# GpSimd's row additions ahead of a tanh: tensor-scalar with a per-partition scalar in place of tensor-tensor with a broadcast operand

## The chip, the cores and the metric

The kernel runs on one core of a Trainium2 chip. The metric is the device time of one execution in microseconds (us), the median of several runs. Beside it stands one execution taken by the hardware profiler, whose span is some microseconds shorter than the timed runs. The engines are called PE (TensorE), ACT (ScalarE), DVE (VectorE), POOL (GpSimd) and SP (SyncE, which issues DMAs). Every tensor is float32.

## What is computed

The input x has 8 batches of 64 x 16 = 1024 tokens with 128 channels. Layer 0 is an attention block with 8 heads, two softmaxes in a row on each score matrix, a feed-forward block and two layer norms. Layer 1 is an additive attention followed by a recurrence. The change is in the additive attention, whose heart is this:

```python
Wi = jnp.einsum('bnd,ed->bne', B, W)
scores = jnp.einsum('d,bijd->bij', v, jnp.tanh(Wi[:, None, :, :] + Wi[:, :, None, :]))
attn = jax.nn.softmax(scores, axis=-1)
```

For each of the 1024 tokens i of a batch, a row of Wi is added to all rows j, the tanh of every sum is taken, and the result is multiplied by v and summed over the 128 channels d. That is 1024 x 1024 x 128 tanh values per batch. The scores are symmetric in i and j, so the kernel computes only the blocks with j not before i, and gets the rest by transposing. After the attention, a linear recurrence through a sigmoid runs over the tokens; it stands at the end of the kernel and is not touched.

## The kernel before

**Tiling.** Channels lie on the 128 partitions and tokens along the free axis. `wiT` holds Wi of one batch in this form, 128 x 1024. Adding row i of Wi to all rows is then adding one column of `wiT`, a value per partition, to a 128 x w piece of `wiT`. The tokens i are cut into 8 tiles `it` of 128. For tile `it` only the w = 1024 − 128·it columns from its diagonal on are computed. Tiles 0 to 3 (w from 1024 to 640) are the wide ones; tiles 4 to 7 are the narrow ones.

**Groups.** `group` (from L930 on) adds the work of one group to the plan. A group takes k rows from each of the four 32-row quarters c of a tile, so 4k rows in all, with k = max(1, 1024 // w): one for the wide tiles, two for w = 512 and 384, four and eight for the last two tiles. Each row drops the columns ahead of its own diagonal (`begin`). A group lives in one of three buffers `th`, each 128 x 4096, and passes three steps:

1. *Fill.* Either ScalarE does addition and tanh in one instruction per row (`tanh_row`, L955, with the row's value as bias), or GpSimd or VectorE does only the additions. GpSimd does them by `add_rows` (L962), one tensor-tensor instruction per quarter c for its k rows, both operands broadcast views of `wiT`. VectorE does them by `add_row` (L958, tensor-scalar, one row each) for k under 4, else by `add_rows`.
2. *Tanh.* If the fill was only additions, ScalarE takes the tanh of the whole group in one instruction (L999).
3. *Product with v.* TensorE multiplies the rows with a pattern of v (L1016) and collects the scores of a tile in `sa`. This gives the `th` buffer free.

**Other work around it.** While batch b is in its layer-1 attention, layer 0 of batch b+1 is computed between: scores on TensorE (L820), exponentials on ScalarE (L823, L836), sums and divisions on VectorE (L827 to L840), and the second division on GpSimd (L843, a tensor-tensor with a broadcast operand, not changed). Transposes (L749) pass through PSUM banks that VectorE empties (L761), and L862 is the product with the values. Only layer 0 of batch 0 at the start, and the attention of batch 7 with the recurrence at the end, stand alone.

**What sets the order.** The kernel adds every piece of work to a `Plan`, with its engine or several engines to choose from, a cost in us for each, a priority and its dependences. `Plan.emit` runs a list scheduler over them when the kernel is built: it always takes the piece that can start earliest by these costs, within a small slack the one with the best priority, and puts it on an engine. So the costs in the table `work` decide which engine fills which group, and the order of every queue is fixed from then on. Pieces on GpSimd and those on VectorE that are marked `port` are planned so that they never overlap. For the wide tiles and the first narrow one, GpSimd is among the choices except for the last three groups of a tile; for the wide tiles, VectorE is among them only in the last batch.

Of the kernel before, what the change touches and what calls it, by code (L numbers as in the profile page):

```python
# [11 lines left out]
ALU = mybir.AluOpType  # L12
# [396 lines left out]
class Plan:  # L409
# [24 lines left out]
    def add(self, where, fn, r=(), w=(), pri=0, mode="full", take=None, give=None, behind=(), wait=(), port=False):  # L434
        n = len(self.ops)
        deps = set()
        for k in r:
            if k in self.writer:
                deps.add(self.writer[k])
        for k in (*w, *wait):  # L440
            if k in self.writer:
                deps.add(self.writer[k])
            deps.update(self.readers.get(k, ()))
        for k in w:
            self.writer[k] = n
            self.readers[k] = []
        for k in r:
            if k not in w:
                self.readers.setdefault(k, []).append(n)
        deps.discard(n)  # L450
        self.ops.append((where, fn, (pri, n), mode, deps, take, give, behind, port))
        self.by.append(None)
        return n
# [107 lines left out]
def fast_path(ctx: ExitStack, tc: tile.TileContext, a: dict, fits):  # L561
# [5 lines left out]
    nc = tc.nc  # L567
# [365 lines left out]
    def group(it, at0, r0, k, wiT, all_wi, L1, ROWS, fillers, chain, left, both):  # L933

        i0 = it * P
        w = N - i0
        g = count.setdefault("group", 0)  # L940
        count["group"] = g + 1
        slot = Bank(*slots)

        begin = [0 if r0 == 0 else 32 * c + r0 for c in range(4)]
        at = [k * sum(w - q for q in begin[:c]) for c in range(5)]

        def rows(c):
            return slot()[:, at[c] : at[c + 1]].rearrange("p (r n) -> p r n", r=k)

        def w_i(c, r=None):  # L950
            j = i0 + 32 * c + r0
            return wiT[:, j : j + k] if r is None else wiT[:, j + r : j + r + 1]

        def tanh_row(c, r):
            nc.scalar.activation(rows(c)[:, r, :], wiT[:, i0 + begin[c] :], AF.Tanh, bias=w_i(c, r))  # L955

        def add_row(c, r):
            nc.vector.tensor_scalar(rows(c)[:, r, :], wiT[:, i0 + begin[c] :], w_i(c, r), None, ALU.add)  # L958

        def add_rows(eng, c):  # L960
            shape = [P, k, w - begin[c]]
            eng.tensor_tensor(  # L962
                rows(c), wiT[:, i0 + begin[c] :].unsqueeze(1).to_broadcast(shape),
                w_i(c).unsqueeze(2).to_broadcast(shape), ALU.add,
            )


        each = [(c, r) for r in range(k) for c in range(4)]
        work = {
            "ACT": [(0.19 + 0.833e-3 * (w - begin[c]), lambda c=c, r=r: tanh_row(c, r)) for c, r in each],  # L970
            "POOL": [
                (0.25 + 1.7e-3 * k * (w - begin[c]), lambda c=c: add_rows(nc.gpsimd, c)) for c in range(4)
            ],
            "DVE": [(0.27 + 0.52e-3 * (w - begin[c]), lambda c=c, r=r: add_row(c, r)) for c, r in each]
            if k < 4
            else [(0.15 + 1.04e-3 * k * (w - begin[c]), lambda c=c: add_rows(nc.vector, c)) for c in range(4)],
        }

        def does(i):
            return lambda e: work[e][i][1]()  # L980

        first = count[chain] = add(
            [(e, work[e][0][0], x) for e, x in fillers], does(0), r=all_wi, w=[("rows", g, 0)], pri=ROWS,
            take=slot, behind=[count[q] for q in (chain, *both) if q in count], port=True,
        )

        def placed(i):
            def where():
                e = plan.by[first]

                return (e, work[e][i][0], -1.0 if e == "DVE" else 0.0) if i < len(work[e]) else None

            return where

        for i in range(1, 4 * k):
            add(placed(i), does(i), w=[("rows", g, i)], pri=ROWS, behind=[first], port=True)
        add(
            lambda: None if plan.by[first] == "ACT" else ("ACT", 0.2 + 0.833e-3 * at[4]),
            lambda _: nc.scalar.activation(slot()[:, : at[4]], slot()[:, : at[4]], AF.Tanh),  # L999
            r=[("rows", g, i) for i in range(4 * k)], w=[("tanh", g)], pri=ROWS - 0.02,  # L1000
        )


        parts = []
        for s0 in range(0, N, 512):
            for c in range(4):
                s, s1 = max(s0, at0 + begin[c]), min(s0 + 512, at0 + w)
                if s < s1:
                    parts.append((c, s0, s, s1))
                    left[c, s0] = left.get((c, s0), 0) + k  # L1010

        def times_v(_):
            for r in range(k):
                for c, s0, s, s1 in parts:
                    left[c, s0] -= 1
                    nc.tensor.matmul(  # L1016
                        sa[32 * c : 32 * c + 32, s:s1], vpat[:, 31 - r0 - r : 63 - r0 - r],
                        rows(c)[:, r, s - at0 - begin[c] : s1 - at0 - begin[c]],
                        start=at0 + r0 + r == 0, stop=left[c, s0] == 0,
                    )  # L1020

        n = -(-w // 512)
        before = ["sa"] if at0 and r0 == 0 else ["sa", "sa narrow"] if at0 else ["sa"] if r0 else []
        after = ["sa narrow"] if at0 and r0 == 0 else [] if r0 or at0 else ["sa"]
        add(
            ("PE", k * (1.67e-3 * (w - begin[0]) + 0.03 * n)), times_v, r=[("tanh", g)] + before,
            w=[("sa", it, r0)] + after, pri=L1, mode="groups", give=slot,
        )  # L1030
        return ("sa", it, r0)
# [11 lines left out]
    def layer1(b):  # L1043
# [19 lines left out]
        for n_pair, pair in enumerate(shared):  # L1063
# [16 lines left out]
            for s, it, at0, r0, k, fillers in sorted(todo):  # L1080
                ROWS = b + (n_pair + s / 33) / len(shared)
                L1 = ROWS - SOON
                keys.append(group(it, at0, r0, k, wiT, all_wi, L1, ROWS, fillers, fills[it < NT // 2], left, fills if r0 == 0 else ()))
# [188 lines left out]
    with tc.tile_pool(name="ps_w", bufs=2, space=PSUM) as ps_w, tc.tile_pool(  # L1272
# [26 lines left out]
        for g in range(NT // 4):  # L1299
            for b in range(NB):  # L1300
# [5 lines left out]
                eng = nc.sync if n % 2 else nc.scalar  # L1306
# [71 lines left out]
```

## Time and profile before

The median of 3 runs is 5963.16 us (5958.27 to 5963.76). The profiled execution has a span of 5955.2 us.

| engine | busy us | share of the span | instructions |
|---|---|---|---|
| PE | 5354.3 | 90% | 38755 |
| ACT | 5339.7 | 90% | 5305 |
| DVE | 4608.0 | 77% | 7127 |
| POOL | 3443.5 | 58% | 2186 |

The instructions that the change can touch, over the whole span:

| what | instructions | busy us | mean ns of one |
|---|---|---|---|
| L962 POOL, additions of a quarter | 1596 | 2397.4 | 1529 |
| L955 ACT, addition and tanh of a row | 3228 | 2434.9 | 821 |
| L999 ACT, tanh of a group | 695 | 1915.0 | 2771 |
| L958 DVE, addition of a row | 1244 | 597.2 | 547 |
| L962 DVE, additions of a quarter | 368 | 402.1 | 1154 |
| L843 POOL, second division | 512 | 997.4 | 1951 |

A busy time is the time in which at least one instruction of the group ran, while the mean is that of one instruction from its start to its end. Neighbours overlap a little, so busy time over count is below the mean. In a line of a group, the part after the second bar is the idle time of that engine just ahead of such instructions, and what ended most of it: "<-PE sa L1016 1008.2" says that the engine stood idle for 1008.2 us until a TensorE instruction of line 1016 was done. In a line of a window, the busy times stand in the order PE, PE's weight loads, DVE, ACT, POOL, with the number of instructions in brackets, and then the granted clock of TensorE and figures for DMA. The chain of waits follows the work that ended last back to the start, and gives each line's share of it.

### The profile page before, as it was taken

How to read it: one execution, taken by the hardware profiler on the slowest of the kernel's cores; microseconds unless marked ns; L12 is line 12 of the kernel's file. 1: busy time of each engine (PE TensorE's matmuls, PEld its weight loads, DVE VectorE, ACT ScalarE, POOL GpSimd, SP SyncE). 2: the span in 40 equal slices, each digit the busy share in tenths (PEclk: the TensorE clock that was granted, in tenths of full speed). 3: DMA queues.
4: the chain of work that ended last, by engine and by line, in shares of the span. 5: the costliest groups of instructions: out<-in, count | busy, mean ns of one | idle time of the engine just before them, and what ended most of it. 6: DMA issues, size and time to landing. Idle time of an engine off the chain costs nothing.

```text
span 5955.2 us, 96887 instructions
## 1 busy us (share of the span) xinstructions
PE 5354.3 (90%) x38755; PEld 3111.3 (52%) x38755; DVE 4608.0 (77%) x7127; ACT 5339.7 (90%) x5305; POOL 3443.5 (58%) x2186
## 2 busy tenths in 40 slices
PE   8989999999989998999999999999998999976667
PEld 5655555555555555455555555555554555532335
DVE  7897787878887778867788778887788777877754
ACT  5549999999998998999998999989999899989983
POOL 2338766786556766587655775568764767620000
PEclk9999999999999999999999999999999999989988
DMA  2000000000000000000000000000000000000001
GB/s 57 1 4 1 1 1 5 5 1 1 1 5 4 1 1 1 6 3 1 1 5 4 1 1 1 5 4 1 1 1 3 3 1 1 1 4 1 1 3 59
DMA packets 24301, 30.42 MB, mean 5 GB/s; under 512 B 2128, under 2 KB 18896, under 8 KB 23840
## 3 DMA queue, kind: packets, MB, share of 16 engines
q1 hardware_dynamic: 18736, 20.65, 1.1%
q8 instruction: 306, 5.01, 0.4%
q10 hardware_dynamic: 4944, 3.16, 0.2%
q14 instruction: 155, 1.27, 0.1%
q0 software_dynamic: 160, 0.33, 0.0%
HBM read 15.74 MB, written 8.39 MB: 4 GB/s over the span
## 4 chain that ended last, share of the span: by engine, by line
PE 52%; ACT 25%; DVE 16%; issue 6%; POOL 0%; DMA 0%; ACTq 0%; DVEq 0%; POOLq 0%
PE sa L1016 21%; ACT th L999 11%; ACT th L955 10%; PE m L862 9%; PE sc L820 9%; PE m L749 5%; DVE th L962 3%; DVE th L958 2%; ACT e L836 2%; ACT sc L823 2%; PE m L1124 2%; DVE aT L761 1%; PE sa L862 1%; DVE stat_e L839 1%; DVE stat_e L827 1%
## 5 line engine op out<-in xcount | busy, mean ns | idle before, releaser
L962 POOL TENSOR_TENSOR th<-wiT 128x1024 f32<-128x1024 f32 (+58 forms) x1596 | 2397.4, 1529 | 1310.8 <-PE sa L1016 1008.2
L955 ACT ACTIVATE th<-wiT 128x733 f32<-128x733 f32 (+61 forms) x3228 | 2434.9, 821 | 188.6 <-PE sa L1016 162.7
L1016 PE MATMUL sa<-th,vpat 128*32 128x512 f32 (+39 forms) x24576 | 2284.3, 474 | 292.7 <-ACT th L999 287.2
L999 ACT ACTIVATE th<-th 128x4096 f32<-128x4096 f32 (+48 forms) x695 | 1915.0, 2771 | 83.3 <-DVE th L958 40.5
L1016 PEld LDWEIGHTS sa<-th,vpat 128*32 128x32 f32 x24576 | 1033.7, 112 | 1352.8 <-issue 549.0
L843 POOL TENSOR_TENSOR e<-e,stat_e 128x1024 f32<-128x1024 f32 x512 | 997.4, 1951 | 882.8 <-DVE stat_e L840 698.2
L820 PE MATMUL sc<-xT,u 128*128 128x512 f32 x2048 | 987.5, 606 | 31.5 <-DVE e L831 28.9
L862 PE MATMUL m<-aT,vp 128*128 128x256 f32 x3664 | 891.9, 391 | 19.6 <-DVE aT L761 15.6
L862 PEld LDWEIGHTS m<-aT,vp 128*128 128x128 f32 x3664 | 677.2, 192 | 278.4 <-issue 109.4
L827 DVE TENSOR_REDUCE stat_e<-sc 128x16 f32<-128x1024 f32 x512 | 619.8, 1210 | 212.6 <-ACT sc L823 211.7
L839 DVE TENSOR_REDUCE stat_e<-e 128x64 f32<-128x1024 f32 x512 | 617.6, 1206 | 163.5 <-ACT e L836 161.4
L958 DVE TENSOR_SCALAR th<-wiT 128x384 f32<-128x384 f32 (+41 forms) x1244 | 597.2, 547 | 189.4 <-PE sa L1016 183.8
L761 DVE COPY aT<-m 128x512 f32<-128x512 f32 x906 | 587.1, 674 | 183.4 <-PE m L749 181.1
L831 DVE TENSOR_TENSOR e<-sc,stat_e 128x1024 f32<-128x1024 f32 x512 | 621.2, 1213 | 19.8 <-DVE stat_e L828 0.5
L749 PE MATMUL m<-ident,e 128*128 128x128 f32 x3796 | 558.7, 282 | 64.0 <-DVE aT L761 34.1
L823 ACT ACTIVATE sc<-sc 128x1024 f32<-128x1024 f32 x512 | 509.4, 1001 | 111.9 <-PE sc L820 111.6
L749 PEld LDWEIGHTS m<-ident,e 128*128 128x128 f32 x3796 | 420.4, 142 | 360.0 <-issue 177.9
L836 ACT ACTIVATE e<-e 128x1024 f32<-128x1024 f32 x512 | 534.1, 1046 | 51.1 <-DVE e L831 50.1
L820 PEld LDWEIGHTS sc<-xT,u 128*128 128x128 f32 x2048 | 357.1, 192 | 344.0 <-issue 288.5
L962 DVE TENSOR_TENSOR th<-wiT 128x1024 f32<-128x1024 f32 (+13 forms) x368 | 402.1, 1154 | 61.3 <-PE sa L1016 61.1
L840 DVE RECIPROCAL stat_e<-stat_e 128x64 f32<-128x64 f32 x512 | 283.2, 553 | 17.6
L718 POOL TENSOR_TENSOR stat<-stat,neg_half 128x4 f32<-128x4 f32 x64 | 67.6, 1056 | 227.7 <-DVE stat L715 225.9
(159 smaller groups left out, 2839.2 us busy)
## 6 DMA issues: line engine op xcount, KB each, us to landing
xT<-in_xt_dram SPq DMA_DIRECT2D x8, 512.0 KB, 3.6
th<-in_x_dram SPq DMA_DIRECT2D x8, 512.0 KB, 6.9
parked<-X SPq DMA_DIRECT2D x16, 256.0 KB, 2.0
xr<-parked SPq DMA_DIRECT2D x8, 512.0 KB, 7.0
out_dram<-ot ACTq DMA_DIRECT2D x8, 256.0 KB, 2.4
out_dram<-ot SPq DMA_DIRECT2D x8, 256.0 KB, 2.4
th<-in_wkn_dram ACTq DMA_DIRECT2D x1, 512.0 KB, 5.2
th<-in_wqn_dram SPq DMA_DIRECT2D x1, 512.0 KB, 5.0
```

Of the source, the lines that this page charges most:

```text
L749: nc.tensor.transpose(bank[:, i * P : (i + 1) * P], s, ident)
L820: nc.tensor.matmul(sc[:, cols], u[:, qt * P : (qt + 1) * P], xT[:, cols], start=True, stop=True)
L827: nc.vector.tensor_reduce(r1, sc.rearrange("p (m g) -> p g m", g=G), AX.X, ALU.add)
L836: add(("ACT", 1.05), lambda _, e=e: nc.scalar.activation(e, e, AF.Exp), r=[ke], w=[ke], pri=L0)
L839: nc.vector.tensor_reduce(r2, e3, AX.X, ALU.add)
L843: nc.gpsimd.tensor_tensor(e3, e3, r2.unsqueeze(2).to_broadcast([P, M, G]), ALU.mult)
L862: nc.tensor.matmul(bank()[:, :256], vp[:, t, :], aT[:, t, :], start=t == 0, stop=t == NT - 1)
L955: nc.scalar.activation(rows(c)[:, r, :], wiT[:, i0 + begin[c] :], AF.Tanh, bias=w_i(c, r))
L958: nc.vector.tensor_scalar(rows(c)[:, r, :], wiT[:, i0 + begin[c] :], w_i(c, r), None, ALU.add)
L962: eng.tensor_tensor(rows(c), wiT[:, i0 + begin[c] :].unsqueeze(1).to_broadcast(shape), w_i(c).unsqueeze(2).to_broadcast(shape), ALU.add,)
L999: lambda _: nc.scalar.activation(slot()[:, : at[4]], slot()[:, : at[4]], AF.Tanh),
L1016: nc.tensor.matmul(sa[32 * c : 32 * c + 32, s:s1], vpat[:, 31 - r0 - r : 63 - r0 - r], rows(c)[:, r, s - at0 - begin[c] : s1 - at0 - begin ...
```

## The change

GpSimd's entry in the table `work` is altered for k under 4, which is every group that GpSimd may take. It now adds row by row with a tensor-scalar instruction, whose second operand is one value per partition, in place of a tensor-tensor whose second operand is a broadcast column. So each instruction reads one stream of elements from SBUF rather than two. `add_row` gets the engine as an argument, so that GpSimd and VectorE share it. The planner's cost of a GpSimd row falls with it, from 1.7 to 0.9 ns an element; the fixed part stays at 0.25 us. Its aim is to make GpSimd's additions shorter, and with the new cost the planner distributes the groups over the engines anew.

```diff
-        def add_row(c, r):
-            nc.vector.tensor_scalar(rows(c)[:, r, :], wiT[:, i0 + begin[c] :], w_i(c, r), None, ALU.add)
+        def add_row(eng, c, r):
+            eng.tensor_scalar(rows(c)[:, r, :], wiT[:, i0 + begin[c] :], w_i(c, r), None, ALU.add)
...
             "POOL": [
-                (0.25 + 1.7e-3 * k * (w - begin[c]), lambda c=c: add_rows(nc.gpsimd, c)) for c in range(4)
-            ],
-            "DVE": [(0.27 + 0.52e-3 * (w - begin[c]), lambda c=c, r=r: add_row(c, r)) for c, r in each]
+                (0.25 + 0.9e-3 * (w - begin[c]), lambda c=c, r=r: add_row(nc.gpsimd, c, r)) for c, r in each
+            ]
+            if k < 4
+            else [(0.25 + 1.7e-3 * k * (w - begin[c]), lambda c=c: add_rows(nc.gpsimd, c)) for c in range(4)],
+            "DVE": [(0.27 + 0.52e-3 * (w - begin[c]), lambda c=c, r=r: add_row(nc.vector, c, r)) for c, r in each]
             if k < 4
             else [(0.15 + 1.04e-3 * k * (w - begin[c]), lambda c=c: add_rows(nc.vector, c)) for c in range(4)],
```

## The prediction

> **What bounds the kernel now.** I read the busy times of the page first, then the slices, a window over the middle, the chain of waits and each engine's waits in that window.
>
> ```profile
> PE 5354.3 (90%) x38755; PEld 3111.3 (52%) x38755; DVE 4608.0 (77%) x7127; ACT 5339.7 (90%) x5305; POOL 3443.5 (58%) x2186
> ```
> Two engines are nearly full, TensorE and ScalarE; GpSimd, whose instructions change, is not. The slices say where it works at all: hardly in the first two of 40, and not in the last four, where batch 7's attention is alone. So the stretch from 480 to 5200 us decides.
>
> ```profile
> 480.00:5200.00 4720.00, 4429.45 (x32656) 2547.74 (x32655) 3710.40 (x5514) 4476.98 (x4414) 3211.52 (x2043) 0.98 0.01 2
> ```
> Of 4720 us, PE is busy 4429 (94%), ACT 4477 (95%), DVE 3710 (79%), POOL 3212 (68%). The chain of waits and the groups of the same stretch:
>
> ```profile
> by line: PE sa L1016 24.3%; ACT th L955 11.6%; PE m L862 11.1%; PE sc L820 8.9%; ACT th L999 8.5%; PE m L749 5.6%; issue 4.0%; DVE th L962 3.2%; ACT e L836 2.2%; ACT sc L823 2.0%; DVE th L958 1.8%; PE m L1124 1.8%; DVE aT L761 1.3%; PE m L7
> ...
> L962 POOL TENSOR_TENSOR th<-wiT 128x1018 f32<-128x1018 f32 (+62 forms) x1556 | 2329.4, 1524 | 782.2 <-PE sa L1016 692.7 <-ACT th L955 40.9 <-DVE wiT L761 16.9
> L955 ACT ACTIVATE th<-wiT 128x308 f32<-128x308 f32 (+62 forms) x2965 | 2255.5, 828 | 146.7 <-PE sa L1016 121.8 <-DVE wiT L761 22.4
> L1016 PE MATMUL sa<-th,vpat 128*32 128x256 f32 (+40 forms) x20992 | 1904.9, 464 | 94.6 <-ACT th L999 89.2 <-ACT th L955 3.8
> L999 ACT ACTIVATE th<-th 128x4096 f32<-128x4096 f32 (+44 forms) x541 | 1487.5, 2756 | 63.5 <-DVE th L962 37.9 <-DVE th L958 21.6 <-POOL th L962 3.0
> ```
> The chain has no GpSimd piece among its leaders. PE never appears as waiting for POOL's rows; the big tanh (L999) waits for them 3 us. POOL itself waits 693 us for TensorE to give a buffer of th back. A faster GpSimd row by itself is therefore worth nearly nothing. What can pay is that, being cheap, GpSimd is given more groups, and ScalarE fewer instructions. TensorE waits for ScalarE 89.2 + 3.8 = 93 us here.
>
> **What the Trainium skill says.** "GPSIMD Engine Reference", section 4.1 (Engine selection), puts two-input elementwise work at about twice VectorE's time, because both inputs go through one read port, and calls one-input work "roughly line-rate"; section 1 gives 1.2 GHz. Line rate is then 0.83 ns an element, an estimate from that page. Section 3.1 has 2.6 cycles an element for two inputs. The trace disagrees in size: its tensor-tensor rows (below) take 1.55 ns, 1.9 cycles. Nearly two cycles for two reads fits the one port all the same. "SBUF — State Buffer", section Who interferes with whom: a GpSimd instruction shuts out VectorE instructions in the two-port mode (tensor-scalar) and those with two SBUF inputs for its whole length, and the other way round. The trace agrees in direction: the same VectorE row addition of 128x1024 takes 1220 ns in the median and 1501 ns in the mean.
>
> **The change, part by part.**
>
> *Price of the new instruction.* The trace has no GpSimd tensor-scalar. The nearest rows:
>
> ```profile
> L962 POOL TENSOR_TENSOR th<-wiT 128x1024 f32<-128x1024 f32 x32 | 59.8, 1891 | 26.5 <-PE sa L1016 20.6 <-DVE wiT L761 5.8
> ...
> L962 POOL TENSOR_TENSOR th<-wiT 128x640 f32<-128x640 f32 x28 | 35.6, 1296 | 26.3 <-ACT th L955 17.7 <-PE sa L1016 8.7
> ```
> (1891 − 1296)/384 = 1.55 ns an element, and 1296 − 640×1.55 = 0.30 us fixed. Lower bound: 0.30 us and the line rate, 0.83 ns. Upper bound: 0.30 us and the full 1.55 ns, as if the second read cost nothing. I take the lower one, since the trace's 1.9 cycles for two reads already looks port-bound. The planner's own figure in the diff, 0.25 us and 0.9 ns, is only what decides the order; for a row of 735 elements it and mine both give 0.91 us.
>
> *What moves.* Counted in the two built programs: GpSimd goes from 1596 additions over 1,262,028 elements per partition to 2428 over 1,785,072 (mean 735). ScalarE's row tanh (L955) goes from 3228 to 2572 instructions, its tanh over a whole group (L999) from 695 to 859. In groups: GpSimd fills 567 in place of 399, ScalarE 517 in place of 681, VectorE 200 in place of 204 of those with few rows. The last batch hardly changes (20 additions become 28), so all of it falls in the stretch.
>
> *GpSimd.* New rows in the stretch: about 2400 × 0.30 + 1,757,000 × 0.83 ns = 720 + 1458 = 2178 us, against 2329. With its other work, 3212 − 2329 = 882 us, it is busy 3060 of 4720. Off the chain both times: worth 0 directly, hidden beside TensorE's 4429 us. At the upper price it is 720 + 2723 + 882 = 4325 us.
>
> *ScalarE.* Its elements stay the same, since each row gets its tanh either way; only fixed costs go. From the group tanh of 4096 elements (3609 ns) and 3072 (2752 ns) the slope is 0.837 ns. Row tanh occupies 2434.9/3228 = 754 ns for 646 elements, so 213 ns of overhead; group tanh 1915.0/695 = 2755 ns for 3095 elements, so 165 ns. Saved: 656 × 0.213 − 164 × 0.165 = 140 − 27 = 113 us.
>
> *Buffers.* No wait is added, but the three th buffers are held for other lengths. A one-row-each group of 791-element rows was filled by GpSimd in 4 × 1.53 = 6.1 us, now 4 × 0.96 = 3.8: 399 groups × 2.3 = 918 us of buffer time less. The 168 groups that come over from ScalarE took 4 × 0.75 = 3.0 us there and now 3.8 plus a 2.8 us tanh: 168 × 3.6 = 605 us more. The net −313 us is 2% of 3 × 4720. Queued behind a waiting GpSimd row are its second divisions (L843), for which TensorE's transposes wait; 68% busy falling to 65% leaves these no later.
>
> *Sum.* ScalarE's row tanh is on the chain for 11.6% of 4720 = 548 us, 24% of its 2255 us. With the order unchanged, 113 × 0.24 = 27 us would be felt. The most that TensorE can regain from ScalarE is its 93 us. The plan is made anew around the freed time, so I go above 27 by a third of the other 66: 27 + 22 = 49 us. A third only, because TensorE's other 4720 − 4429 − 93 = 198 us of waits (VectorE's evictions of banks mostly) are untouched and are what it meets next. At the end, the matmul columns left after the last layer-0 matmul fall from 568,480 to 564,848; ScalarE at 0.837 ns passes those 3632 in 3 us. Together 52 us: 5963 − 52 = 5911.
>
> **The rivals.**
>
> *All of it arrives* (ScalarE is the true bound): 5963 − 113 = 5850. For: ACT is the fuller engine, 95%. Against: it waits 122 us for TensorE's buffers in the same stretch, and TensorE has only 93 us to win from it.
>
> *Nothing arrives*: TensorE paces, and ScalarE's freed time becomes more waiting for th buffers: 5963 − 3 = 5960. For: 52% of the chain is TensorE. Against: 25% is ScalarE.
>
> *The new order is worse*: every queue is fixed at build time, and moving 168 of some 1380 groups moves evictions and transposes against each other. Should TensorE's 198 us of other waits grow by half, +99 − 52 = +47: 6010. For: those waits come from close meetings in the list. Against: port time on GpSimd falls from 2329 to 2178 us, so VectorE is shut out less.
>
> *GpSimd becomes a bound*: at 1.55 ns it needs 4325 us, late against an order made for 0.9 ns. If only half of its former idle time (4720 − 3212 = 1508) can be squeezed out, the stretch is 4325 + 754 = 5079, or 359 longer: 6322. Against: 1.9 cycles for two inputs. Between, at 1.2 ns, it needs 720 + 2108 + 882 = 3710 us, which with the same 754 still fits in 4720.
>
> **How the numbers follow.** Forecast 0.58, all of it 0.10, nothing 0.13, worse order 0.11, GpSimd bound 0.08. Faster is 0.58 + 0.10 = 0.68, same 0.13, slower 0.11 + 0.08 = 0.19. The range runs from the full saving, 5850, to 5990, part of the way to the worse order; it leaves out GpSimd as the bound (0.08), the farther half of the worse order, and a few chances in a hundred below 5850.
>
> **What will show it.** GpSimd's addition at 1024 elements near 0.30 + 0.85 = 1.15 us proves the price; near 1.9 us disproves it. ACT's busy total should fall from 5340 to about 5227, with 2572 row tanh and 859 group tanh, and TensorE's waits for ScalarE in the middle from 93 towards 45. If ACT's idle time for th buffers rises from 122 us by most of the 113, nothing arrived. If TensorE waits on VectorE grow well over 198 us, the order is worse; if the group tanh waits for GpSimd rows by much more than 3 us, the price was wrong. The weakest step is the share of 113 us that the re-made order lets through.

## The result and the profile after

The changed kernel takes 8205.75 us in the median of 4 runs (8199.98 to 8209.1), against 5962.42 us (5958.27 to 5963.76, 4 runs): 1.3763 times as long, with a 95% interval from 1.3739 to 1.3787. The prediction was 5911 us, with 5990 us as the upper end; it named the direction wrongly.

From the page before, the chain of waits and the groups of the product with v and of the group tanh over the whole span:

```profile
PE 52%; ACT 25%; DVE 16%; issue 6%; POOL 0%; DMA 0%; ACTq 0%; DVEq 0%; POOLq 0%
...
L1016 PE MATMUL sa<-th,vpat 128*32 128x512 f32 (+39 forms) x24576 | 2284.3, 474 | 292.7 <-ACT th L999 287.2
L999 ACT ACTIVATE th<-th 128x4096 f32<-128x4096 f32 (+48 forms) x695 | 1915.0, 2771 | 83.3 <-DVE th L958 40.5
```
From the page after, the busy times, GpSimd's and the clock's slices, the chain of waits, and the groups that answer to those:

```profile
PE 6035.8 (74%) x38755; PEld 3393.5 (41%) x38755; DVE 4590.8 (56%) x7091; ACT 5289.1 (64%) x4813; POOL 6268.0 (76%) x3018
...
POOL 3378988999878988698977988879898698875101
PEclk9988889888898888988888888898888988889988
...
POOL 37%; PE 27%; ACT 18%; issue 11%; DVE 6%; DMA 0%; POOLq 0%; ACTq 0%; DVEq 0%
POOL th L958 33%; PE sa L1018 16%; ACT th L1001 14%; POOL e L843 4%; PE sc L820 3%; ACT th L955 3%; PE m L749 2%; PE m L862 2%; DVE stat_e L839 1%; PE sa L862 1%; DVE th L958 1%; ACT e L836 1%; DVE aT L761 1%; DVE stat_e L840 1%; PE m L799 0%
...
L958 POOL TENSOR_SCALAR th<-wiT 128x689 f32<-128x689 f32 (+58 forms) x2428 | 5222.9, 2170 | 1061.8 <-PE sa L1018 657.2
L1018 PE MATMUL sa<-th,vpat 128*32 128x512 f32 (+36 forms) x24576 | 2766.3, 553 | 1794.3 <-ACT th L1001 1685.7
L1001 ACT ACTIVATE th<-th 128x4096 f32<-128x4096 f32 (+49 forms) x859 | 2384.5, 2787 | 2378.3 <-POOL th L958 2349.3
```
GpSimd's additions have grown from 2397 to 5223 us. GpSimd is the fullest engine and leads the chain with 37%, where it had none. The waits hand the delay on in one line each: the group tanh (L1001 here) waits 2349 us for GpSimd's rows, where it waited 3.0 us for them in the stretch that the prediction looked at, and the product with v (L1018) waits 1686 us for the group tanh, where it waited 287. ScalarE did lose the instructions as counted (5289 us busy in place of 5340), but that no longer matters. The granted clock of TensorE is lower too, 0.87 in the mean in place of 0.97, and TensorE is busy for 74% of the span in place of 90%; whether the one follows from the other was not tested.

How long one instruction takes, by shape, in the changed kernel:

```profile
L958 POOL TENSOR_SCALAR th<-wiT 128x640 f32<-128x640 f32 x24 | 47.0, 1974 | 28.3 <-PE sa L1018 28.2
L958 POOL TENSOR_SCALAR th<-wiT 128x1024 f32<-128x1024 f32 x16 | 45.4, 2852 | 13.7 <-DVE wiT L761 13.7
```
At 1024 elements it is 2852 ns, against 1891 for the tensor-tensor. A straight line through all 2428 gives 0.36 us and 2.46 ns an element. The instruction that reads one stream of elements takes 50% longer here than the one that reads two.

### The profile page after: what moved, and what is told of

Read it like the earlier page. It is cut to its first block, busy times and chain, and to the rows that moved or that the text cites. A ratio compares the mean times of both kernels' runs of the same rounds, so it can differ in the third digit from the quotient of the medians.

```text
span 8207.3 us, 97533 instructions
## 1 busy us (share of the span) xinstructions
PE 6035.8 (74%) x38755; PEld 3393.5 (41%) x38755; DVE 4590.8 (56%) x7091; ACT 5289.1 (64%) x4813; POOL 6268.0 (76%) x3018
## 4 chain that ended last, share of the span: by engine, by line
POOL 37%; PE 27%; ACT 18%; issue 11%; DVE 6%; DMA 0%; POOLq 0%; ACTq 0%; DVEq 0%
POOL th L958 33%; PE sa L1018 16%; ACT th L1001 14%; POOL e L843 4%; PE sc L820 3%; ACT th L955 3%; PE m L749 2%; PE m L862 2%; DVE stat_e L839 1%; PE sa L862 1%; DVE th L958 1%; ACT e L836 1%; DVE aT L761 1%; DVE stat_e L840 1%; PE m L799 0%
## 5 line engine op out<-in xcount | busy, mean ns | idle before, releaser
L958 POOL TENSOR_SCALAR th<-wiT 128x689 f32<-128x689 f32 (+58 forms) x2428 | 5222.9, 2170 | 1061.8 <-PE sa L1018 657.2
L1018 PE MATMUL sa<-th,vpat 128*32 128x512 f32 (+36 forms) x24576 | 2766.3, 553 | 1794.3 <-ACT th L1001 1685.7
L1001 ACT ACTIVATE th<-th 128x4096 f32<-128x4096 f32 (+49 forms) x859 | 2384.5, 2787 | 2378.3 <-POOL th L958 2349.3
L1018 PEld LDWEIGHTS sa<-th,vpat 128*32 128x32 f32 x24576 | 1179.0, 123 | 3076.6 <-ACT th L1001 2030.7
L955 ACT ACTIVATE th<-wiT 128x835 f32<-128x835 f32 (+61 forms) x2572 | 1876.3, 790 | 169.6 <-PE sa L1018 165.5
L749 PE MATMUL m<-ident,e 128*128 128x128 f32 x3796 | 624.7, 305 | 195.4 <-POOL e L843 158.6
L958 DVE TENSOR_SCALAR th<-wiT 128x384 f32<-128x384 f32 (+57 forms) x1208 | 621.0, 580 | 215.5 <-PE sa L1018 213.2
L749 PEld LDWEIGHTS m<-ident,e 128*128 128x128 f32 x3796 | 472.1, 155 | 558.2 <-issue 224.7
L962 DVE TENSOR_TENSOR th<-wiT 128x1024 f32<-128x1024 f32 (+19 forms) x368 | 382.8, 1100 | 175.3 <-PE sa L1018 168.6
L869 DVE TENSOR_TENSOR zs<-m,zs 128x256 f32<-128x256 f32 x198 | 81.4, 411 | 238.3 <-PE m L862 238.0
```

Source lines behind the costliest of these rows:

```text
L749: nc.tensor.transpose(bank[:, i * P : (i + 1) * P], s, ident)
L958: eng.tensor_scalar(rows(c)[:, r, :], wiT[:, i0 + begin[c] :], w_i(c, r), None, ALU.add)
L1018: nc.tensor.matmul(sa[32 * c : 32 * c + 32, s:s1], vpat[:, 31 - r0 - r : 63 - r0 - r], rows(c)[:, r, s - at0 - begin[c] : s1 - at0 - begin ...
```

## Experiments

The ratios below are to the kernel before on the same chip, with a 95% interval. "Old plan" is the order of every queue in the kernel before, "new plan" that of the changed kernel. Adding lines moves line numbers: the GpSimd additions are at L958, L960 or L964, the group tanh between L999 and L1012.

### What one GpSimd instruction costs by itself

```diff
+    for w in (1024, 512):
+        s, d = src[:, :w], dst[:, :w]
...
+            nc.gpsimd.tensor_scalar(d, s, col, None, ALU.add)
+            nc.gpsimd.tensor_scalar(d, s, 1.5, None, ALU.add)
+            nc.gpsimd.tensor_scalar(d, s, col, 2.0, ALU.add, ALU.mult)
+            nc.gpsimd.tensor_tensor(d, s, s, ALU.add)
+            nc.gpsimd.tensor_tensor(d, s, col.to_broadcast([P, w]), ALU.add)
+            nc.gpsimd.tensor_copy(d, s)
```
Each stands three times in a row, at L1272, L1274, L1276, L1278, L1280 and L1282 in this order; `col` is one value per partition.

Expected: 

> The kernel before, with 36 extra GpSimd instructions on a scratch tile near the end, where GpSimd is otherwise idle (nothing is left out). Price theory (the instruction itself is slow): tensor-scalar with a per-partition scalar takes 0.36 + 1.024 x 2.46 = 2.9 us at 1024 elements here too. Contention theory (VectorE shut it out through the shared port): well below, near 1.15 us, since VectorE is lightly used here. Tensor-tensor with the broadcast column 1.9 us in both. With an immediate in place of the column: about 1.1 us if the fetch of the scalar is what costs, 2.9 us if the routine is slow whatever the operand.

Measured, groups of GpSimd near the end (the kernel as a whole took 5959.51 us):

```profile
L1272 POOL TENSOR_SCALAR dst<-src 128x1024 f32<-128x1024 f32 x3 | 8.6, 2862 | 0.2
L1274 POOL TENSOR_SCALAR dst<-src 128x1024 f32<-128x1024 f32 x3 | 8.4, 2814 | 0.3
L1280 POOL TENSOR_TENSOR dst<-src 128x1024 f32<-128x1024 f32 x3 | 5.7, 1892 | 0.2
...
L1276 POOL TENSOR_SCALAR dst<-src 128x1024 f32<-128x1024 f32 x3 | 3.5, 1161 | 0.3
...
L1282 POOL COPY dst<-src 128x1024 f32<-128x1024 f32 x3 | 3.1, 1038 | 0.2
L1276 POOL TENSOR_SCALAR dst<-src 128x512 f32<-128x512 f32 x3 | 2.3, 768 | 0.3
...
L1282 POOL COPY dst<-src 128x512 f32<-128x512 f32 x3 | 2.1, 695 | 0.2
```
The lone addition is as slow here as in the changed kernel, and a constant in place of the column (L1274) changes nothing. VectorE was not as idle as expected, though: in the stretch of this list it was busy for 36 of 61 us, and nearly all the time beside five of the six lone additions of 1024 elements. So this list alone doesn't exclude that VectorE held GpSimd up. But the same instruction with a second operation, a multiplication, takes 1161 ns, with VectorE's instructions beside it too: (1161 − 768)/512 = 0.77 ns an element and 0.37 us fixed. A second list asked which second operations do that.

Expected: 

> The kernel before with a second price list of GpSimd tensor-scalar forms near the end, nothing left out. If a second operation, of whatever kind, is what selects the fast routine: every form with two operations near 1.16 us at 1024 elements, every form with one near 2.85 us, also for multiplication and maximum. If it is a special routine for add-then-multiply: add-then-add and multiply-then-add near 2.85 us.

Measured, again near the end:

```profile
L1272 POOL TENSOR_SCALAR dst<-src 128x1024 f32<-128x1024 f32 x2 | 7.4, 3710 | 0.1
L1284 POOL TENSOR_SCALAR dst<-src 128x1024 f32<-128x1024 f32 x2 | 7.4, 3704 | 0.2
L1280 POOL TENSOR_SCALAR dst<-src 128x1024 f32<-128x1024 f32 x2 | 5.8, 2888 | 0.2
L1282 POOL TENSOR_SCALAR dst<-src 128x1024 f32<-128x1024 f32 x2 | 5.7, 2868 | 0.2
L1272 POOL TENSOR_SCALAR dst<-src 128x512 f32<-128x512 f32 x2 | 4.2, 2116 | 0.2
...
L1274 POOL TENSOR_SCALAR dst<-src 128x1024 f32<-128x1024 f32 x2 | 2.5, 1235 | 0.2
L1278 POOL TENSOR_SCALAR dst<-src 128x1024 f32<-128x1024 f32 x2 | 2.3, 1154 | 0.2
L1276 POOL TENSOR_SCALAR dst<-src 128x1024 f32<-128x1024 f32 x2 | 2.2, 1088 | 0.2
```
In this list L1272 is add then add, L1284 add then maximum, L1280 a lone multiplication, L1282 a lone maximum; L1274 and L1276 are add then multiply (with two columns, with two constants), L1278 multiply then add. The second of the two lone maxima ran with no VectorE instruction beside it and took 2838 ns, and the two add-then-maximum instructions (3709 and 3698 ns) had one beside them for at most 63 ns: contention is out as the reason for such prices, and the lone addition has that of the lone maximum. Among the tensor-scalar forms tried, the pairs of an addition and a multiplication are fast, in either order and with either kind of operand, and nothing else. So "a second operation" was too wide, and "add-then-multiply" too narrow. Why the pair is special stays open; the runs only show that it is.

### Price and order apart

Old plan, new instruction:

```diff
-                (0.25 + 1.7e-3 * k * (w - begin[c]), lambda c=c: add_rows(nc.gpsimd, c)) for c in range(4)
+                (0.25 + 1.7e-3 * k * (w - begin[c]), lambda c=c: add_by_rows(c)) for c in range(4)
...
+        def add_by_rows(c):
+            for r in range(k):
+                add_row(c, r, nc.gpsimd)
```

Expected: 

> The kernel before with its own plan and costs, only each of GpSimd's additions done by tensor-scalar. Price theory: 1736 rows over 1262 thousand elements take 625 + 3105 = 3730 us in place of 2397, 4530 us with its other work in the middle stretch of 4720; with half to two thirds of its former 1508 us idle time kept, 6500 to 6750 us in all. Order theory (the plan made anew did the harm): under 6060 us.

Measured: 6664.57 us, 1.1173 (1.1154 to 1.1191). From its page:

```profile
L958 POOL TENSOR_SCALAR th<-wiT 128x613 f32<-128x613 f32 (+53 forms) x1736 | 3715.7, 2158 | 1003.3 <-PE sa L1020 684.9
L1003 ACT ACTIVATE th<-th 128x4096 f32<-128x4096 f32 (+48 forms) x695 | 1919.3, 2777 | 783.4 <-POOL th L958 736.6
```
GpSimd's additions are busy 3715.7 us, against 3730 expected, and the time is in the range of the price theory: the instruction alone, in an unchanged order, costs 700 us, and the group tanh waits 737 us for GpSimd's rows.

New plan, old instruction (on GpSimd each row is a tensor-tensor with the broadcast column):

```diff
-            eng.tensor_scalar(rows(c)[:, r, :], wiT[:, i0 + begin[c] :], w_i(c, r), None, ALU.add)
+            src = wiT[:, i0 + begin[c] :]
+            if eng is nc.gpsimd:
+                eng.tensor_tensor(rows(c)[:, r, :], src, w_i(c, r).to_broadcast([P, w - begin[c]]), ALU.add)
+            else:
+                eng.tensor_scalar(rows(c)[:, r, :], src, w_i(c, r), None, ALU.add)
```

Expected: 

> The changed kernel, same order of every queue, but each GpSimd row is a tensor-tensor with the broadcast column again. Price theory: 2400 x 0.27 + 1757 x 1.59 = 3440 us plus 882 us of other work, 4320 us; with the idle time of the changed kernel, 961 us, the stretch is 5285 us, so 6300 to 6550 us in all. Order theory: near 8200 us. If it comes out below 5960 us the new distribution was good and the price alone spoiled it.

Measured: 6610.14 us, 1.1082 (1.1064 to 1.1101). The order that was made for 0.9 ns an element is costly even with the old 1.6 ns, somewhat more than expected. So price and order both count. By a count explained further down, VectorE was held up for 321 us by GpSimd's additions here, more than in any other run; how much of the time that cost was not tested.

New instruction, planner told its true price:

```diff
-                (0.25 + 0.9e-3 * (w - begin[c]), lambda c=c, r=r: add_row(nc.gpsimd, c, r)) for c, r in each
+                (0.36 + 2.46e-3 * (w - begin[c]), lambda c=c, r=r: add_row(nc.gpsimd, c, r)) for c, r in each
```

Expected: 

> The changed kernel, but the planner is told 0.36 us and 2.46 ns an element for a GpSimd row. It then gives GpSimd 924 thousand elements in place of 1785 thousand, and ScalarE 3756 row tanh. Price theory: GpSimd is busy about 2730 + 882 us in the middle and no longer late; ScalarE has about 90 us more than in the kernel before, of which a quarter to all is felt: 5985 to 6060 us. Contention theory (the long instruction holds the port against VectorE): over 6200 us even with the right cost.

Measured: 5930.32 us, 0.9944 (0.9928 to 0.9961). The slow instruction does no harm once the plan allows for it, so the harm lies in the mismatch of price and order. That this kernel is even faster than before, although ScalarE is busy 5424 us in place of 5340, was not expected by either theory. The gain of 34 us is about what a new order can make by itself, as a run below shows, so it has no known cause; but had ScalarE's load been all that counts, the kernel would have been slower.

### The instruction that was meant: add, then multiply by 1.0

```diff
-            eng.tensor_scalar(rows(c)[:, r, :], wiT[:, i0 + begin[c] :], w_i(c, r), None, ALU.add)
+            src = wiT[:, i0 + begin[c] :]
+            if eng is nc.gpsimd:
+                eng.tensor_scalar(rows(c)[:, r, :], src, w_i(c, r), 1.0, ALU.add, ALU.mult)
+            else:
+                eng.tensor_scalar(rows(c)[:, r, :], src, w_i(c, r), None, ALU.add)
```
Everything else is as in the changed kernel, new plan included. The multiplication leaves the values as they are.

Expected: 

> The changed kernel with the same order of every queue, but each GpSimd tensor-scalar has a second operation, a multiplication by 1.0, in place of none. In the price list this form took 1.16 us at 1024 elements and 0.77 us at 512, near what the planner had been told. Price theory with the reasoning of the prediction (ScalarE's saved 113 us count): 5850 to 5945 us, GpSimd's additions about 2428 x 0.37 + 1785 x 0.77 = 2270 us. Rival, made from the run with the true cost, which was faster than the kernel before although ScalarE had more to do (groups that pass through GpSimd hold a buffer longer and lose time): 5970 to 6060 us.

Measured: 5734.53 us, 0.9621 (0.9608 to 0.9634). This is the fastest kernel of the study, 225 us below the one before, and better than expected.

```profile
PE 5271.5 (92%) x38755; PEld 3081.7 (54%) x38755; DVE 4453.5 (78%) x7091; ACT 5232.8 (91%) x4813; POOL 3210.0 (56%) x3018
...
PE 59%; ACT 24%; DVE 11%; issue 5%; POOL 1%; DMA 0%; ACTq 0%; DVEq 0%; POOLq 0%
...
L960 POOL TENSOR_SCALAR th<-wiT 128x689 f32<-128x689 f32 (+58 forms) x2428 | 2160.9, 911 | 1436.3 <-PE sa L1022 1027.7
```
A row takes 911 ns in the mean, the very price that the prediction had used (0.91 us), and ScalarE is down by 5340 − 5233 = 107 us, near the 113 foretold. VectorE's busy time has fallen too, by 155 us, with nearly the same instructions.

With the planner told this form's exact price:

```diff
-                (0.25 + 0.9e-3 * (w - begin[c]), lambda c=c, r=r: add_row(nc.gpsimd, c, r)) for c, r in each
+                (0.37 + 0.77e-3 * (w - begin[c]), lambda c=c, r=r: add_row(nc.gpsimd, c, r)) for c, r in each
```

Expected: 

> The changed kernel with the two-operation form, and the planner told what it takes, 0.37 us and 0.77 ns an element in place of 0.25 and 0.9. Rows of 735 elements cost 0.94 against 0.91 us, and it gives GpSimd 1767 against 1785 thousand elements. If only the size of the price matters: within 20 us of 5735. If any new order moves the time by itself: outside that.

Measured: 5765.00 us, 0.9675 (0.9662 to 0.9688), 30 us slower than with the cruder price. With nearly the same work (ScalarE busy 5238 us), the plan's order alone thus moves the time by some 30 us, and no difference of that size between two plans can be put down to a cause.

### Which half of the 225 us comes from where

The old plan with the fast form leaves ScalarE's work and every order as before. It is the run with the old plan and the new instruction, with the second operation added on GpSimd:

```diff
-            eng.tensor_scalar(rows(c)[:, r, :], src, w_i(c, r), None, ALU.add)
+            eng.tensor_scalar(rows(c)[:, r, :], src, w_i(c, r), 1.0, ALU.add, ALU.mult)
```

Expected: 

> The kernel before with its own plan (same order of every queue, same ScalarE work), only GpSimd's rows done by the two-operation tensor-scalar: 1736 x 0.37 + 1262 x 0.77 = 1614 us of GpSimd in place of 2397. If the 225 us that the changed kernel gains with this form come from ScalarE's saved instructions: within 25 us of 5960. If they come from GpSimd's shorter instructions (VectorE shut out less, buffers free sooner) in any order: 5800 to 5880 us. Parts of both: between.

Measured: 5839.49 us, 0.9798 (0.9785 to 0.9812). So 120 us come from the shorter instruction in an unchanged order, about half of the 225, although the time lies in the range of the second reading. The other 105 us (5839 to 5735; with the other new plan, 5765, it is 75) come with the new distribution, near what ScalarE saves.

Busy times from the first product with v to the last matmul of layer 0, the kernel before and then the old plan with the fast form:

```profile
479.00:5284.00 4805.00, 4504.10 (x33165) 2589.02 (x33163) 3782.19 (x5671) 4553.08 (x4521) 3242.53 (x2063) 0.98 0.01 2
```
```profile
481.00:5169.00 4688.00, 4470.30 (x33164) 2574.73 (x33162) 3623.11 (x5679) 4544.28 (x4518) 2416.54 (x2194) 0.99 0.01 2
```
The work is the same, as the counts of PE, DVE and ACT show. ScalarE is as busy as before; VectorE is busy 159 us less. In these stretches TensorE's waits for VectorE fall from 193 to 106 us, those for ScalarE stay (101 and 105). How VectorE lost time, the layer norms' scalings of 128x128 show, first in the kernel before, then in the old plan with the fast form:

```profile
L722 DVE TENSOR_SCALAR B<-X,stat 128x128 f32<-128x128 f32 x128 | 74.4, 644 | 2.7 <-POOL stat L718 2.7
L722 DVE TENSOR_SCALAR X<-X,stat 128x128 f32<-128x128 f32 x128 | 73.9, 639 | 0.9 <-POOL stat L718 0.9
```
```profile
L722 DVE TENSOR_SCALAR B<-X,stat 128x128 f32<-128x128 f32 x128 | 52.5, 474 | 3.5 <-POOL stat L718 3.5
L722 DVE TENSOR_SCALAR X<-X,stat 128x128 f32<-128x128 f32 x128 | 50.6, 457 | 0.9 <-POOL stat L718 0.9
```
An undisturbed one takes 343 ns. To see what disturbs them, I counted in the traces those of VectorE's scalings and row additions that start while GpSimd is in one of its fill instructions, and how much longer they take than undisturbed (343 ns for a scaling; 212 ns + 0.525 ns an element for tensor-scalar rows, the line through those that ran beside no GpSimd instruction; 165 ns + 1.02 ns for tensor-tensor rows). "Held" are those more than 100 ns longer, or half of what was left of GpSimd's instruction where that is less.

| kernel, old plan throughout | GpSimd's instruction | started | held | longer in all, us | kernel, us |
|---|---|---|---|---|---|
| before | tensor-tensor | 185 | 174 | 173 | 5959 |
| fast form | add then multiply | 171 | 115 | 52 | 5839 |
| fast form, slowed by zeros | both kinds | 271 | 152 | 79 | 5851 |
| fast form, slowed by copies | both kinds | 333 | 178 | 80 | 5855 |
| before, in halves | tensor-tensor | 276 | 257 | 154 | 5953 |

Under a tensor-tensor, VectorE's instructions of these kinds wait in 174 of 185 cases, in the mean for most of what GpSimd still had to do. The scalings and tensor-scalar rows do so very evenly: all 118 that started with more than 0.3 us of GpSimd's instruction left came out longer by that remainder less 0.13 to 0.27 us. The last three rows are the runs that were to tell this reading from another, that groups filled sooner give buffers back sooner.

Slowed by zeros, and the same with a copy of a piece of `wiT`:

```diff
+                if c or r:
+                    late = (0.82 * n - (100.0 if k == 1 else 235.0)) * 4 * k / (4 * k - 1)
+                    size = min(n, max(16, int((late - 270.0) / 0.665)))
+                    nc.gpsimd.memset(rows(c)[:, r, :size], 0.0)
                 add_row(c, r, nc.gpsimd)
```

Expected, zeros: 

> The old plan with the two-operation tensor-scalar, but GpSimd is made about as slow as with tensor-tensor again: ahead of each row but the first of a group it fills part of that row with zeros (an instruction that writes SBUF and reads nothing), 0.55 us in the mean, which the row then overwrites. If the 120 us that this plan gained came from groups being filled sooner: back to 5920 to 5970 us. If it came from GpSimd holding the shared read port for less time against VectorE: 5830 to 5870 us, with VectorE busy near 4440 us as without the zeros.

Expected, copies: 

> The same with a copy of a piece of wiT (read and write) in place of the zeros, for the same lost time. Filled sooner: 5920 to 5970 us, the same as with the zeros. Read port: 5920 to 5970 us here, while the zeros stay at 5830 to 5870 us, and VectorE busy near 4600 us here alone.

Measured: 5850.66 us, 0.9816 (0.9802 to 0.9829), and 5854.74 us, 0.9824 (0.9810 to 0.9837). From the pages, the fast form alone, then zeros, then copies:

```profile
L960 POOL TENSOR_SCALAR th<-wiT 128x613 f32<-128x613 f32 (+53 forms) x1736 | 1543.8, 905 | 1603.3 <-PE sa L1024 1221.8
```
```profile
L960 POOL TENSOR_SCALAR th<-wiT 128x613 f32<-128x613 f32 (+53 forms) x1736 | 1575.1, 908 | 1385.2 <-PE sa L1029 957.5
L970 POOL MEMSET th<- 128x16 f32 (+45 forms) x1337 | 725.8, 543 | 2.9 <-PE sa L1029 1.7
```
```profile
L960 POOL TENSOR_SCALAR th<-wiT 128x613 f32<-128x613 f32 (+53 forms) x1736 | 1575.2, 908 | 1373.1 <-PE sa L1029 939.8
L970 POOL COPY th<-wiT 128x16 f32<-128x16 f32 (+45 forms) x1337 | 758.4, 567 | 2.3 <-PE sa L1029 0.9
```
GpSimd spends 1575 + 726 = 2301 us on filling with the zeros, nearly the 2397 of before. From the start of the first to the end of the last instruction, the filling of one group took 7.35 us in the mean before, 5.72 with the fast form, 7.31 with the zeros and 7.40 with the copies. VectorE is busy 4473 and 4479 us, near the 4440 of the fast form. So the groups are filled as slowly as before again, and only 11 to 15 of the 120 us are given back. Filling sooner is therefore not what gained them.

The copies were expected to take the gain away by reading, and did not. They do hold VectorE up: all 15 scalings and tensor-scalar rows that started with more than 0.3 us of a copy left came out longer by that remainder less 0.13 to 0.27 us, as under a tensor-tensor, and so did all 16 under a fill with zeros. But most copies are short, 0.57 us in the mean: of 94 such VectorE instructions, 79 started with less than 0.3 us of one left and lost 1 us together, and in all the copies cost VectorE's rows and scalings 14 us. The expectation had gone by the copies' total time and not by how long one lasts, so this run can't tell reading from writing.

The tensor-tensor cut in two:

```diff
+            for a, z in ((0, n // 2), (n // 2, n)) if eng is nc.gpsimd else ((0, n),):
+                shape = [P, k, z - a]
```

Expected: 

> The kernel before with its own plan, each GpSimd tensor-tensor cut into two halves of its columns, so that GpSimd needs about 1596 x 0.27 = 430 us more, but no instruction holds VectorE up for longer than half as long. If what counts is how long one GpSimd instruction shuts VectorE out: the 167 us by which VectorE's row additions and scalings were stretched fall to about 100, and the time to 5890 to 5930 us, although GpSimd has more to do. If what counts is how soon GpSimd fills a group: 5965 to 6040 us.

Measured: 5953.25 us, 0.9992 (0.9983 to 1.0000), neither of the two.

```profile
L964 POOL TENSOR_TENSOR th<-wiT 128x512 f32<-128x512 f32 (+58 forms) x3192 | 2655.3, 866 | 1126.8 <-PE sa L1018 971.2
```
An instruction that starts under one loses 0.56 us in the mean in place of 0.94, but 276 start under one in place of 185, so the sum falls only from 173 to 154 us (the 167 of the expectation is the 173, with a cruder line for the tensor-scalar rows). GpSimd's fill grows by 258 us and costs nothing that can be measured. Over the five kernels of the table, all with one plan and the same ScalarE work, time rises with VectorE's lost time and not with GpSimd's. That leaves VectorE's being held up as the likely cause of the 120 us, though no run changes that alone. Time goes by VectorE's loss only while GpSimd keeps up: the sixth kernel with this plan, the one with the slow tensor-scalar, takes 6665 us with 138 us lost by VectorE, because there the group tanh waits for GpSimd itself.

### Does GpSimd's speed count when it has few groups

The run with the true cost, its order kept (the planner still reckons with 2.46 ns), with the two edits shown above for GpSimd's row: tensor-tensor, then the fast form.

Expected, tensor-tensor: 

> The order of the run with the true cost (few groups on GpSimd), but its rows done by tensor-tensor, 1.6 in place of 2.46 ns an element. If GpSimd's own speed is off the chain once the plan allows for it: within 15 us of 5930. If the shorter fill counts (buffers free sooner): 5850 to 5910 us.

Expected, fast form: 

> The same order again, with the two-operation tensor-scalar, 0.77 ns an element, a third of what the plan allows for. Off the chain: within 15 us of 5930. Shorter fill counts: faster than the run with tensor-tensor in this order.

Measured: 5950.66 us, 0.9982 (0.9974 to 0.9990), and 5898.55 us, 0.9901 (0.9886 to 0.9916), beside 5930.32 with the slow tensor-scalar. GpSimd's rows with the slow tensor-scalar, the tensor-tensor and the fast form:

```profile
L958 POOL TENSOR_SCALAR th<-wiT 128x504 f32<-128x504 f32 (+43 forms) x1272 | 2726.2, 2158 | 1051.8 <-PE sa L1018 554.0
```
```profile
L960 POOL TENSOR_TENSOR th<-wiT 128x504 f32<-128x504 f32 (+43 forms) x1272 | 1777.0, 1422 | 1350.0 <-PE sa L1022 858.7
```
```profile
L960 POOL TENSOR_SCALAR th<-wiT 128x504 f32<-128x504 f32 (+43 forms) x1272 | 1135.2, 909 | 1497.4 <-PE sa L1022 976.1
```
The quicker tensor-tensor (1777 us of GpSimd) is slower in all than the lone addition (2726 us), so the first run fits neither of its readings. The second came out as "shorter fill counts" had it, but that reading can't be right if the tensor-tensor, a shorter fill than the lone addition, loses time. VectorE's lost time under GpSimd's rows, by the count above, is 101 us with tensor-tensor, 80 with the lone addition and 35 with the fast form: the times stand in the same order.

## Why the prediction was wrong

**The price of the instruction** is the step that failed: "I take the lower one, since the trace's 1.9 cycles for two reads already looks port-bound." The price was 0.36 us and 2.46 ns, above the upper bound as well. That bound, the tensor-tensor's own 1.55 ns, assumed that one input can't cost more than two. Nothing in the trace tied one instruction's price to the other's. The Trainium skill ("GPSIMD Engine Reference", section 4.1 Engine selection), which calls one-input work "roughly line-rate", is right here for the copy ((1038 − 695)/512 = 0.67 ns) and for an addition with a multiplication (0.77), and wrong for every tensor-scalar with one operation; the measurements decide. An operation that no trace shows should have kept an open upper end. 0.08 for "GpSimd becomes a bound" and a range that left it out were far too sure. The sign that the prediction named for a wrong price, a group tanh that waits for GpSimd's rows by much more than 3 us, is the one that came.

**That rival's arithmetic** was near. With the measured price the new rows in the stretch take 2400 × 0.36 + 1,757,000 × 2.46 ns = 864 + 4322 = 5186 us, and with 882 of other work and 754 of idle time kept 6822; 5963 + 6822 − 4720 = 8065 us, against 8206. The work was right: from 483 to 7537 us of the changed kernel, up to the last matmul of layer 0, GpSimd is busy 6042 us, where this sum has 6068. That half of the idle time of 1508 us would stay was a guess; 7054 − 6042 = 1012 us stayed.

**What moves**, the counts of instructions and groups, came out exactly, being read from the programs; only the buffer sum takes all 168 groups as ScalarE's, where 164 were and 4 were VectorE's, which changes little. **ScalarE's saving**, 113 us, was 51 in the changed kernel and 107 with the fast form.

**The share that arrives** failed as a size. The fast form at the assumed price gained 225 us, not 52. From the old plan with the fast form to the two new plans with it, the time fell by 105 and 75 us and ScalarE's busy time by 99 and 94. So much of ScalarE's part seems to have come through, more than 27 us plus a third of 66; its share of the chain of waits, 24%, was no measure of what less of its work is worth. Other effects of the new order, some 30 us, are in these figures, and no run takes them out.

**GpSimd's shorter rows, "worth 0 directly"**, were worth 120 us. The prediction knew that GpSimd shuts VectorE out and put no number on it; the 281 ns between median and mean of one row addition stood before it. TensorE's "other" 198 us of waits, VectorE's mostly, that it called "untouched" were what fell: those for VectorE went from 193 to 106 us in the stretches above. The "Buffers" step, which found 2%, agrees with the two slowed runs.

**Worse order** as a rival had a real size, about 30 us between two plans of nearly equal costs.

## What to carry to other kernels

Before an instruction form is used by the hundreds, time that very form once, operations and operand kinds included, in an idle corner of the kernel; a cost told to a static planner that is wrong by a factor of 2.5 can cost far more than the instruction itself: here 2240 us in an order made for 0.9 ns, where the same planner, told the true price, made the slow form harmless (0.9944). And an engine with no share in the chain of waits can still be worth shortening, if its instructions hold another engine up: look in that other engine for instructions whose mean lies well above their undisturbed duration.

## What the runs showed of the hardware

- GpSimd tensor-scalar on float32, 128x1024: 2.8 to 2.9 us for one operation (add, multiply or maximum), 3.7 us for add-add and add-maximum, 1.09 to 1.24 us for an addition and a multiplication in either order. Copy 1.04, tensor-tensor 1.89, fill with a constant 0.95 us.
- How GpSimd holds VectorE's tensor-scalars up (the row additions and scalings counted above). The Trainium skill ("SBUF — State Buffer", section Who interferes with whom) has the port kept for the whole instruction. Of those that started with more than 0.3 us of GpSimd's instruction left, held to its end (longer by that remainder less 0.13 to 0.27 us) were 118 of 118 under tensor-tensor, 15 of 15 under copies, 16 of 16 under fills and 83 of 92 under the fast form, so the traces agree for these. VectorE's tensor-tensor rows, with two inputs, were held under copies (21 of 24), not under fills (0 of 6).
- The lone tensor-scalar is different. In the changed kernel, all 123 VectorE tensor-scalars whose start plus 0.2 us fell in the first 35% of such a GpSimd instruction were held, but only until about 44% of it had passed; of those between 45% and 70%, 133 of 153 ran unhindered; of those between 70% and 90%, all 133 were held to its end. Its price of 2.46 ns an element and that of add-add, (3710 − 2116)/512 = 3.1 ns, are about three and four times the 0.77 ns of the fast pair. Both would fit an instruction that goes over its elements in several passes; no run tests that.
